# Halved, timed and held-back weight loads, fp32 edge sums for the first group and no filler products, in a graph network on one core

## The chip, the core and the metric

The kernel runs on one NeuronCore of a Trainium2 chip. The metric is the device time of one execution in microseconds (us); less is better. Before the change it is 2111.45 us, the median of three runs (2111.43 to 2111.92). Engines have short names here: PE is TensorE (PEld its loads of stationary operands), DVE is VectorE, ACT is ScalarE, POOL is GpSimd and SP is SyncE, whose queue issues all transfers.

## The reference

There are 128 graphs of 128 nodes with 256 features each, and an integer adjacency matrix per graph. Two blocks follow each other, each on normalised input and each added to its input:

```
h = relu(layernorm(x));  A = (adj != 0)
for i in 0..2:                                  # gated graph network
    aggr = A^T (h @ weight[i])
    gi = aggr @ w_ih.T + b_ih;  gh = h @ w_hh.T + b_hh
    r, z = sigmoid(...);  n = tanh(i_n + r * h_n)
    h = (1 - z) * n + z * h
x = x + h
h = relu(layernorm(x));  Wh = h @ W             # attention
e = leaky_relu(s_row + s_col),  s = Wh.sum(-1);  e = -inf where adj == 0
x = x + softmax(e) @ Wh
```

Inputs and outputs are fp32.

## The kernel before

The graphs go through in 32 groups of four. A group passes three GRU layers and then the attention block. A layer needs the edge sums of its state (A times h, `edge_sums`), and twelve gate products with weights that are composed once at the start: w_ih times each layer's message weight (L443, one compose product per 256 or 512 columns) gives `s_x0` to `s_x2`, and w_hh gives `s_hh`. The gate products use sums and differences of 128-wide blocks (`block_sums` for weights, `node_sums` for data), so seven block products stand for eight. PE's `L693` rows are the gate products of layers 0 and 1, `L700` those of layer 2.

All work is first recorded as nodes, with an engine, an estimated duration, dependences and a due time (`op`, L68). `Plan.run` then plays a schedule: each engine takes, of the nodes that can start first, the one with the smallest rank, and the order it finds is the order in which every engine's instructions are issued. Each engine works through its queue strictly in that order. So a changed estimate or due time moves instructions on all engines. Buffers come from small pools: PSUM has eight banks, of which two, called `misc`, serve short jobs such as transposes, edge sums and composes; a product into a bank waits until the bank's last content was copied out by ACT or DVE.

The start (`weights`, L378 on): SP loads w_ih (768 KB) in one transfer, the first group's rows, w_hh (768 KB), the message weights (256 KB each), adjacency blocks (256 KB) and more rows (512 KB). PE transposes the weights in blocks of 128 (`turned`, L348, three transposes into one bank; L430 for message weights), DVE or ACT copy them out (L355), composes follow. Two products of the identity (L313) fill two banks before that and are used for nothing else; they are called dummy products below. DVE takes the statistics of the rows (L512, L519), POOL the inverse root (L525, L526), DVE the shift `nm` (L528), ACT applies them (L534). DVE turns adjacency into bf16 zeros and ones (L905); the integer block has a single buffer, so the next adjacency transfer waits for that step.

The edge sums multiply by A, which is exact in bf16. The fp32 state is split into three bf16 parts whose sum is exact: for row-form states `parts_of` (POOL, L595 and L598) makes the second and third part, and each sum is three bf16 products (L635).

The end: the last two groups' attention has short steps on all engines. In group 30 ACT takes exponentials (L1010), PE transposes them (L1028), ACT copies (L1030), PE sums weighted rows (L649), ACT copies (L654), PE multiplies by W (L1041) and DVE scales and adds (L1046). The last group is handled in two halves of two graphs: PE transposes h (L1069), ACT copies (L1072), PE multiplies by W (L1078), ACT copies (L1081), and in `by_graph` follow exponentials (L1010), transposes (L1094), DVE copies (L1096), products (L1098) and the final sums (L1101), each graph written out on its own (L1104).

Between these stand filler products. `warm` (L487 to L503) records, for steps of the last two groups, a product with the step's result and then products of the identity with itself, all into bank `x_n` after the last gates; nothing reads them. They are recorded with `late=True`, which is a due time after all others, so that PE takes them only where the planner sees it idle. In the profile they are the rows of L499.

Of the kernel before, what the change touches and what calls it, by code (L numbers as in the profile page):

```python
# [16 lines left out]
P = 128  # L17
G = 4
EPS = 1e-5
ALPHA = 0.2  # L20
SETS = 4
EARLY = 3
ENDING = 2
EARLY_Z = 2
SLOT = 18150
MARGIN = 7000
GATES = 18150
BIG = 3.0e38
# [10 lines left out]
class Plan:  # L39
# [27 lines left out]

    def op(self, eng, ns, fn, reads=(), writes=(), room=(), due=None, mark=None, late=False,  # L68
           turn=None, two=False, lag=None):

        i, deps = len(self.nodes), set()
        for b in room:
            if b.prev is not None:
                deps.update(a[0] for a in b.prev.accesses)
        for is_write, group in ((False, reads), (True, writes)):
            for item in group:  # L80
                b, lo, hi = item if isinstance(item, tuple) else (item, 0, 1 << 30)
                for j, w, l, h in b.accesses:
                    if (w or is_write) and l < hi and lo < h:
                        deps.add(j)
                if is_write and b.prev is not None:
# [12 lines left out]
        self.nodes.append([eng, ns, fn, deps, free, 10 ** 9 if late else self.due if due is None else due,  # L98
                           two or eng == "POOL", self.LAG[eng] if lag is None else lag])
# [114 lines left out]
def kernel(  # L214
# [80 lines left out]
    def ap(b):  # L295
        return phys[(b.tag,) + b.slot]
# [32 lines left out]

    def load(dst, get, src, ns=100):  # L330
        op("SP", ns, lambda: nc.sync.dma_start(get(dst), src), [], [dst])

# [7 lines left out]
    def turned(src, dst, evict):  # L340

        for k in range(KD):
            for a in range(2):
                ps = bank()

                def turn(k=k, a=a, ps=ps):
                    for c in range(3):
                        nc.tensor.transpose(flat(ps)[:, c * P:(c + 1) * P],  # L348
                                            nat(src)[:, 3 * a + c, k * P:(k + 1) * P], ident)
                op("PE", 330, turn, [src], [ps])  # L350
                to_sbuf(evict[(2 * k + a) % len(evict)], 3 * P, ps, dst[k], 3 * P * a)

# [24 lines left out]
    def weights():  # L377
# [4 lines left out]
        def square(b):  # L382
            return plain(b).rearrange("p (k e) -> p k e", k=KD)

        def load_msg(layer):
            op("SP", 1300, lambda: nc.sync.dma_start(
                square(w_msg[layer]), weight[layer].rearrange("(k p) e -> p k e", p=P)),
               [], [w_msg[layer]])


        plan.due = -10 ** 6
        load(w_ih_nat, nat, w_ih.rearrange("(c p) e -> p c e", p=P), 4000)
        load_msg(0)
        plan.due = 10 ** 9
        load(w_hh_nat, nat, w_hh.rearrange("(c p) e -> p c e", p=P), 4000)
        load_msg(1)
        for t, src in (("bias_i", b_ih), ("bias_h", b_hh)):
            load(W[t], ap, src.rearrange("(c p) -> p c", p=P), 500)

# [20 lines left out]
        for layer in range(L):  # L420
# [4 lines left out]
            for e in range(KD):  # L425
# [7 lines left out]
                to_sbuf("ACT", D, ps, wT, half * GN + e * D)  # L433
            if layer == 0:
                load_msg(2)
            w_x = homes[layer]
            for k in range(KD):
                for g0, gn in ((0, 512), (512, 3 * D - 512)):
# [10 lines left out]
                    to_sbuf("DVE", gn, ps, w_x[k], g0)  # L449
            block_sums(w_x, W[f"s_x{layer}"], *(("POOL", 1000) if layer else ("DVE", 560)))  # L450

        tmp = [buf("e"), buf("e"), buf("eT")]
        for t, i, b in ((tmp[0], 0, b_ih), (tmp[1], 0, b_hh), (tmp[2], 0, b_hh), (tmp[2], 1, b_ih)):
            n = t is tmp[2]
            op("SP", 500, lambda t=t, i=i, b=b, n=n: nc.sync.dma_start(
                plain(t)[:, i * D:(i + (1 if n else 2)) * D],
                (b[2 * D:] if n else b[:2 * D]).rearrange("(o c) -> o c", o=1)
                .to_broadcast([P, D if n else 2 * D])), [], [(t, i, i + 1)])  # L460

# [24 lines left out]

    def warm(t, ns, get=None):  # L487


        if plan.group < NG - 2:  # L490
            return
        if not after_gates:
            phase_now, plan.phase = plan.phase, len(turns)
            after_gates.append(buf("x_n"))
            plan.phase = phase_now
        b = after_gates[0]

        def product(what):
            nc.tensor.matmul(flat(b)[:, :what.shape[1]], ident, what, start=False, stop=False,  # L499
                             skip_group_check=True)  # L500
        op("PE", 60, lambda: product(get() if get else plain(t)[:, :P]), [t, b], [], late=True)
        for _ in range(ns // 224):
            op("PE", 224, lambda: product(ident), [t, b], [], late=True)  # L503

    after_gates = []

    def normed(src, dst, lo=0, hi=G):
# [3 lines left out]
        for b in range(lo, hi):  # L511
            op("DVE", 415, lambda b=b: nc.vector.bn_stats(ap(st)[:, b, :], ap(src)[:, b, :]),  # L512
               [(src, b, b + 1)], [(st, b, b + 1)])
            if dst is not src and plan.group == NG - 1:
                warm((st, b, b + 1), 330, lambda b=b: ap(st)[:, b, :])

# [3 lines left out]
        op("DVE", 160 * (hi - lo), aggr, [st], [mv])  # L520
        if dst is not src and plan.group == NG - 1:
            warm(mv, 1100, lambda: ap(mv)[:, lo, :])

        def rstd():
# [5 lines left out]
           [mv, rs], [nm])  # L530
        if dst is not src and plan.group == NG - 1:
            warm(nm, 440, lambda: ap(nm)[:, part])
        for b in range(lo, hi):
# [4 lines left out]
    def flat(b):  # L538
        return ap(b).rearrange("p q n -> p (q n)")
# [86 lines left out]
    def edge_sums(parts, a, dst):  # L626

        part, reads = parts
# [267 lines left out]
    def group(g):  # L896
# [3 lines left out]
        rows0, at, a, hT = buf("rows"), buf("at"), buf("a"), buf("hT")  # L900
        op("SP", 100, lambda: nc.sync.dma_start(ap(rows0), x[graphs].rearrange("b n d -> n b d")),
           [], [rows0])
        op("SP", 100, lambda: nc.sync.dma_start(ap(at), adj[graphs].rearrange("b n m -> n b m")),
           [], [at])
        op("DVE", 420, lambda: nc.vector.tensor_scalar(ap(a), ap(at), 0.0, None,  # L905
# [31 lines left out]
    def attention(g, a, x1, h1, lo, hi):  # L937
# [8 lines left out]
        for b in range(lo, hi):  # L946
            warm((h1, b, b + 1), 440, lambda b=b: ap(h1)[:, b, :8])
            hw = buf("hw")
# [47 lines left out]
        else:  # L996
# [5 lines left out]
           [e], [top])  # L1002
        warm(top, 110, lambda: small(top))
        op("DVE", 150, lambda: nc.vector.tensor_scalar(
            small(low), small(top), -BIG / 1e3, -1.0, op0=OP.max, op1=OP.mult), [top], [low])
        warm(low, 330 * n, lambda: small(low))

# [145 lines left out]
```

## Time and profile before

| | us |
|---|---|
| median of the runs | 2111.45 |
| profiled execution | 2111.13 |
| its span, first to last instruction | 2109.1 |
| PE busy | 2098.9 |
| DVE busy | 1670.6 |
| ACT busy | 1592.1 |
| POOL busy | 940.9 |

The profile's page gives busy times, a chain of work that ended last (followed back from the last instruction), and the costliest groups of instructions. Its trace can be asked for the chain in order of time (start, length, what), for a timeline (start, length, engine, line, operation, output and input, and in brackets the idle time before it and what ended that), and for busy times by stretch. The granted PE clock is 1.000 in the whole span, and the 16 transfer engines moved 137.22 MB at a mean of 65 GB/s, but 145 GB/s in the first fortieth.

| stretch, us | PE busy | DVE busy | ACT busy | GB/s |
|---|---|---|---|---|
| 0 to 5 | 3.64 | 0.09 | 1.28 | 157 |
| 5 to 10 | 3.37 | 2.59 | 0.96 | 348 |
| 10 to 15 | 5.00 | 3.90 | 4.44 | 279 |
| 15 to 20 | 4.27 | 4.99 | 1.03 | 244 |
| 20 to 25 | 4.95 | 2.78 | 2.15 | 95 |
| 25 to 30 | 3.60 | 4.86 | 4.35 | 195 |

### The profile page before, as it was taken

Reading aid. Unit: us, or ns where it says so; the run is one execution under the profiler, and the core shown is the slowest. Engines: PE = TensorE matmul, PEld = TensorE weight load, DVE = VectorE, ACT = ScalarE, POOL = GpSimd, SP = SyncE. Lnnn points to the kernel's source line nnn. Section 1 sums busy time; section 2 is a strip of 40 time slices with the busy share of each in tenths; the row PEclk is TensorE's granted clock in tenths of the full one; section 3 lists DMA queues with packets and bytes.
Section 4 is the critical chain, followed back from the end, with each engine's and each line's share of the span. In section 5 each row is a group of like instructions: output and inputs, shape, how many; then the busy total and the mean of one; then the engine's idle time right before and its main releaser. Section 6 shows DMA issues by size and latency. Waiting matters only on the chain.

```text
span 2109.1 us, 34171 instructions
## 1 busy us (share of the span) xinstructions
PE 2098.9 (100%) x12536; PEld 1877.7 (89%) x12536; DVE 1670.6 (79%) x3365; ACT 1592.1 (75%) x2849; POOL 940.9 (45%) x885
## 2 busy tenths in 40 slices
PE   9999999999999999999999999999999999999999
PEld 7888888898888998898988889988889988988889
DVE  7777888887877888877888778878777887878777
ACT  5567878777877777777778787777777777776775
POOL 5544544445443445544354434454444444335330
PEclk9999999999999999999999999999999999999999
DMA  4222223323333222333222332223332223312321
GB/s 145 46 51 46 55 57 75 61 58 68 68 73 76 51 64 65 68 81 66 58 58 68 73 77 59 56 70 69 73 73 53 59 60 78 68 48 47 79 66 36
DMA packets 365143, 137.22 MB, mean 65 GB/s; under 512 B 296368, under 2 KB 364720, under 8 KB 364976
## 3 DMA queue, kind: packets, MB, share of 16 engines
q1 hardware_dynamic: 364976, 135.05, 29.0%
q8 instruction: 98, 1.61, 0.3%
q14 instruction: 69, 0.57, 0.1%
HBM read 45.36 MB, written 16.78 MB: 29 GB/s over the span
## 4 chain that ended last, share of the span: by engine, by line
PE 97%; DVE 1%; DMA 1%; ACT 0%; issue 0%; SPq 0%; DVEq 0%
PE y_rz L693 16%; PE q_rz L693 10%; PE x_rz L693 10%; PE y_n L693 8%; PE y_rz L700 8%; PE misc L635 6%; PE x_n L693 5%; PE q_rz L700 5%; PE q_n L693 5%; PE x_rz L700 5%; PE misc L1041 5%; PE y_n L700 4%; PE x_n L700 3%; PE q_n L700 3%; PE misc L649 2%; PE x_n L499 1%
## 5 line engine op out<-in xcount | busy, mean ns | idle before, releaser
L595 POOL TENSOR_TENSOR r<-rows 128x512 f32<-128x512 f32 x128 | 139.1, 1107 | 270.8 <-ACT rows L578 183.3
L732 ACT COPY t_rz<-y_rz 128x512 f32<-128x512 f32 x192 | 112.5, 586 | 178.1 <-PE y_rz L693 89.9
L620 POOL TENSOR_TENSOR pl<-d,pl 128x512 bf16<-128x512 f32 x64 | 74.9, 1173 | 296.5 <-ACT pl L618 296.2
L742 DVE TENSOR_TENSOR t_rz<-t_rz,q_rz 128x512 f32<-128x512 f32 x192 | 131.3, 684 | 92.9 <-ACT t_rz L732 53.7
L693 PE MATMUL y_rz<-hs,s_hh 128*128 128x256 f32 x768 | 197.6, 380 | 0.3 <-ACT t_rz L732 0.3
L693 PE MATMUL y_rz<-gs,s_x 128*128 128x256 f32 x768 | 197.1, 379 | 0.0
L667 POOL TENSOR_TENSOR hs<-hT,hs 128x256 f32<-128x256 f32 x96 | 81.7, 851 | 240.8 <-PE q_n L700 172.5
L663 POOL TENSOR_TENSOR hs<-hT 128x512 f32<-128x512 f32 x96 | 130.2, 1356 | 96.6 <-ACT hT L578 32.1
L693 PEld LDWEIGHTS y_rz<-gs,s_x 128*128 128x128 f32 x768 | 145.9, 190 | 19.8
L693 PEld LDWEIGHTS y_rz<-hs,s_hh 128*128 128x128 f32 x768 | 143.1, 190 | 19.7 <-issue 1.0
L598 POOL TENSOR_TENSOR p<-r 128x512 bf16<-128x512 f32 x128 | 154.9, 1230 | 0.0
L742 DVE TENSOR_TENSOR t_n<-t_n,q_n 128x512 f32<-128x512 f32 x192 | 131.3, 684 | 21.4 <-ACT t_n L732 8.7
L693 PE MATMUL x_rz<-hT,s_hh 128*128 128x256 f32 x512 | 131.5, 379 | 0.0
L693 PE MATMUL x_rz<-aT,s_x 128*128 128x256 f32 x512 | 131.4, 379 | 0.0
L512 DVE BATCH_NORM_STATS2 st<-rows 128x6 f32<-128x256 f32 x128 | 45.2, 414 | 101.3 <-DMA rows<-in_x_dram 101.2
L638 ACT COPY aT<-misc 128x512 f32<-128x512 f32 x192 | 111.8, 584 | 15.2 <-PE misc L635 11.3
L815 DVE TENSOR_TENSOR d<-hT,u 128x512 f32<-128x512 f32 x128 | 110.7, 865 | 10.9 <-ACT u L812 10.8
L693 PE MATMUL y_n<-hs,s_hh 128*128 128x256 f32 x384 | 114.4, 379 | 0.0
L693 PE MATMUL y_n<-gs,s_x 128*128 128x256 f32 x384 | 114.2, 379 | 0.0
L1041 PE MATMUL misc<-w,uT 128*128 128x256 f32 x480 | 113.1, 380 | 0.3 <-ACT uT L654 0.3
L615 POOL TENSOR_TENSOR d<-hT,pl 128x512 f32<-128x512 f32 x64 | 91.3, 1428 | 45.4 <-ACT pl L613 39.6
L693 PEld LDWEIGHTS x_rz<-aT,s_x 128*128 128x128 f32 x512 | 97.2, 190 | 13.2
(279 smaller groups left out, 6540.2 us busy)
## 6 DMA issues: line engine op xcount, KB each, us to landing
rows<-in_x_dram SPq DMA_DIRECT2D x32, 512.0 KB, 4.1
x<-in_x_dram SPq DMA_DIRECT2D x32, 512.0 KB, 3.9
out_dram<-x SPq DMA_DIRECT2D x31, 512.0 KB, 2.9
at<-in_adj_dram SPq DMA_DIRECT2D x32, 256.0 KB, 2.8
plT<-pl SPq DMA_TRANSPOSE x186, 3.5
peT<-pe SPq DMA_TRANSPOSE x60, 3.1
rz<-in_L_gnn_w_ih_dram SPq DMA_DIRECT2D x1, 768.0 KB, 5.0
rz<-in_L_gnn_w_hh_dram SPq DMA_DIRECT2D x1, 768.0 KB, 7.6
```

The lines of the kernel that those rows point to most:

```text
L595: op("POOL", 1106, lambda part=part: nc.gpsimd.tensor_tensor(ap(r1)[:, part], ap(rows)[:, part], top(rows)[:, part], OP.subtract), [(rows, ...
L598: op("POOL", 1050, lambda part=part: nc.gpsimd.tensor_tensor(ap(p3)[:, part], ap(r1)[:, part], top(r1)[:, part], OP.subtract), [(r1, n, n ...
L615: op("POOL", 1150, lambda k=k, r=r: nc.gpsimd.tensor_tensor(ap(r), ap(hT)[:, k], part(pl, k, 0), OP.subtract), [(hT, 2 * k, 2 * k + 2), (p ...
L635: nc.tensor.matmul(flat(ps)[:, b * N:(b + 1) * N], part(i, b, k), ap(a)[:, b, :], start=(i == 0), stop=(i == 2))
L638: op("ACT", 590, lambda k=k, ps=ps: nc.scalar.copy(ap(dst)[:, k, :], flat(ps)), [ps], [(dst, 2 * k, 2 * k + 2)])
L663: op(eng, cost, lambda: sub(ap(w)[:, 0:2, :], blocks()[:, 1::2, :], blocks()[:, 0:2, :], OP.subtract), [t], [(w, 0, 2)], two=True)
L693: nc.tensor.matmul(ap(bank)[:, half, :], ap(w)[:, i - 1, q, :], source(t, sums), start=(first and c == 0 and m == 0), stop=False, skip_gro ...
L700: nc.tensor.matmul(ap(bank)[:, m, half * P:(half + len(chunk)) * P], source(t, sums)[:, m * N:(m + 1) * N], ap(w)[:, i - 1, q:q + len(chun ...
L732: op("ACT", 590, lambda: nc.scalar.copy(ap(t), ap(y)), [y], [t], mark=mark)
L742: op("DVE", 690, lambda: nc.vector.tensor_tensor(ap(t), ap(t), ap(q), OP.add), [q], [t])
L815: op("DVE", 690, lambda j=j, d=d, cols=cols: nc.vector.tensor_tensor(ap(d), ap(hT)[:, j, :], ap(u)[:, cols], OP.subtract), [(hT, lo, hi), ...
L1041: nc.tensor.matmul(ap(ps)[:, b, :], ap(uT)[:, k, (m + b) * N:(m + b + 1) * N], ap(w1)[:, k, :], start=(k == 0), stop=(k == KD - 1))
```

## The change

Four things are changed. (1) w_ih is loaded in two transfers of 384 KB, and each transpose group needs only its half; `turned` takes the halves as the outer loop. (2) Loads are recorded with an estimate by size (`KB` = 3 ns per KB, and 3300 ns until they land) instead of a fixed one, for weights and for the first four groups' rows and adjacency. The second message weight gets an early due time; the third, the bias rows and the attention weight are recorded as depending on composed weights (`behind`), which holds back their place in SP's queue. (3) The first group's layer-0 edge sums are fp32 products of the rows with an fp32 copy of A, made by DVE (`whole_sums`), without the split into three parts. (4) `warm` and all its calls are gone.

```diff
-    def load(dst, get, src, ns=100):
-        op("SP", ns, lambda: nc.sync.dma_start(get(dst), src), [], [dst])
+    def load(dst, get, src, kb, behind=()):
+        op("SP", kb * KB, lambda: nc.sync.dma_start(get(dst), src), behind, [dst], lag=3300)
...
-        for k in range(KD):
-            for a in range(2):
+        for a in range(2):
+            for k in range(KD):
...
-                op("PE", 330, turn, [src], [ps])
-                to_sbuf(evict[(2 * k + a) % len(evict)], 3 * P, ps, dst[k], 3 * P * a)
+                op("PE", 330, turn, [(src, a, a + 1)], [ps])
+                to_sbuf(evict[k % len(evict)], 3 * P, ps, dst[k], 3 * P * a)
...
-        plan.due = -10 ** 6
-        load(w_ih_nat, nat, w_ih.rearrange("(c p) e -> p c e", p=P), 4000)
+        plan.due = -10 ** 9
+        for a in range(2):
+            part = slice(3 * a, 3 * a + 3)
+            op("SP", 384 * KB, lambda part=part: nc.sync.dma_start(
+                nat(w_ih_nat)[:, part], w_ih.rearrange("(c p) e -> p c e", p=P)[:, part]),
+               [], [(w_ih_nat, a, a + 1)], lag=3300)
         load_msg(0)
         plan.due = 10 ** 9
-        load(w_hh_nat, nat, w_hh.rearrange("(c p) e -> p c e", p=P), 4000)
+        load(w_hh_nat, nat, w_hh.rearrange("(c p) e -> p c e", p=P), 768)
+        plan.due = -10 ** 8
         load_msg(1)
+        plan.due = 10 ** 9
...
-            if layer == 0:
-                load_msg(2)
...
+            if layer == 0:
+                load_msg(2, [W["s_x0"]])
...
-                .to_broadcast([P, D if n else 2 * D])), [], [(t, i, i + 1)])
+                .to_broadcast([P, D if n else 2 * D])), [W["s_x1"]], [(t, i, i + 1)])
...
-        load(W["w1"], ap, w_att.rearrange("(k p) e -> p k e", p=P), 1300)
+        load(W["w1"], ap, w_att.rearrange("(k p) e -> p k e", p=P), 256, [W["s_x1"]])
...
-    def warm(t, ns, get=None):
...
-            warm((h1, b, b + 1), 440, lambda b=b: ap(h1)[:, b, :8])
...
+    def whole_sums(rows, a32, a, dst):
+        op("DVE", 420, lambda: nc.vector.tensor_copy(ap(a32)[:, :, :N], ap(a)), [a], [a32])
+        for k in range(KD):
+            ps = buf("misc")
+            def edges(k=k, ps=ps):
+                for b in range(G):
+                    nc.tensor.matmul(flat(ps)[:, b * N:(b + 1) * N], ap(rows)[:, b, k * P:(k + 1) * P],
+                                     ap(a32)[:, b, :N], start=True, stop=True)
+            op("PE", 880, edges, [rows, a32], [ps], [dst])
+            op("ACT", 590, lambda k=k, ps=ps: nc.scalar.copy(ap(dst)[:, k, :], flat(ps)),
+               [ps], [(dst, 2 * k, 2 * k + 2)])
...
-                parts = parts_of(rows0)
+                parts = parts_of(rows0) if g >= WHOLE else (rows0, buf("r1"))
```

More of the change, by code (lines that the diff above doesn't have):

```diff
@@ L21 @@
 SETS = 4
+WHOLE = 1
 EARLY = 3
@@ L26 @@
 MARGIN = 7000
+TIMED = 4
+KB = 3
 GATES = 18150
@@ L66, in buf, with op @@
         return b
-    def op(self, eng, ns, fn, reads=(), writes=(), room=(), due=None, mark=None, late=False,
+    def op(self, eng, ns, fn, reads=(), writes=(), room=(), due=None, mark=None,
            turn=None, two=False, lag=None):
@@ L97, in op @@
             b.left += 1
-        self.nodes.append([eng, ns, fn, deps, free, 10 ** 9 if late else self.due if due is None else due,
+        self.nodes.append([eng, ns, fn, deps, free, self.due if due is None else due,
                            two or eng == "POOL", self.LAG[eng] if lag is None else lag])
@@ L383, in square, with load_msg @@
             return plain(b).rearrange("p (k e) -> p k e", k=KD)
[L385 to L388, printed above, removed]
-        plan.due = -10 ** 6
-        load(w_ih_nat, nat, w_ih.rearrange("(c p) e -> p c e", p=P), 4000)
+        def load_msg(layer, behind=()):
+            load(w_msg[layer], square, weight[layer].rearrange("(k p) e -> p k e", p=P), 256,
+                 behind)
+        plan.due = -10 ** 9
[4 more added lines that the diff above has]
+               [], [(w_ih_nat, a, a + 1)], lag=3300)
         load_msg(0)
         plan.due = 10 ** 9
-        load(w_hh_nat, nat, w_hh.rearrange("(c p) e -> p c e", p=P), 4000)
+        load(w_hh_nat, nat, w_hh.rearrange("(c p) e -> p c e", p=P), 768)
+        plan.due = -10 ** 8
         load_msg(1)
+        plan.due = 10 ** 9
         for t, src in (("bias_i", b_ih), ("bias_h", b_hh)):
-            load(W[t], ap, src.rearrange("(c p) -> p c", p=P), 500)
+            load(W[t], ap, src.rearrange("(c p) -> p c", p=P), 100)
         def half_bias():
@@ L456, in weights @@
             n = t is tmp[2]
-            op("SP", 500, lambda t=t, i=i, b=b, n=n: nc.sync.dma_start(
+            op("SP", 150 * KB * (1 if n else 2), lambda t=t, i=i, b=b, n=n: nc.sync.dma_start(
                 plain(t)[:, i * D:(i + (1 if n else 2)) * D],
                 (b[2 * D:] if n else b[:2 * D]).rearrange("(o c) -> o c", o=1)
-                .to_broadcast([P, D if n else 2 * D])), [], [(t, i, i + 1)])
+                .to_broadcast([P, D if n else 2 * D])), [W["s_x1"]], [(t, i, i + 1)])
         def halves(t, j):
@@ L484, in weights @@
         to_sbuf("ACT", D, ps, W["w1_sum"], 0)
-    def warm(t, ns, get=None):
[L490 to L505, printed above, removed]
     def normed(src, dst, lo=0, hi=G):
@@ L513, in normed @@
                [(src, b, b + 1)], [(st, b, b + 1)])
-            if dst is not src and plan.group == NG - 1:
-                warm((st, b, b + 1), 330, lambda b=b: ap(st)[:, b, :])
         def aggr():
@@ L520, in normed @@
         op("DVE", 160 * (hi - lo), aggr, [st], [mv])
-        if dst is not src and plan.group == NG - 1:
-            warm(mv, 1100, lambda: ap(mv)[:, lo, :])
         def rstd():
@@ L530, in normed @@
            [mv, rs], [nm])
-        if dst is not src and plan.group == NG - 1:
-            warm(nm, 440, lambda: ap(nm)[:, part])
         for b in range(lo, hi):
@@ L626, in edge_sums @@
     def edge_sums(parts, a, dst):
+        if isinstance(parts[0], Buf):
+            whole_sums(*parts, a, dst)
+            return
         part, reads = parts
@@ L900, in group @@
         rows0, at, a, hT = buf("rows"), buf("at"), buf("a"), buf("hT")
[L901 to L904, printed above, removed]
+        for t, src, kb in ((rows0, x[graphs].rearrange("b n d -> n b d"), 512),
+                           (at, adj[graphs].rearrange("b n m -> n b m"), 256)):
+            if g < TIMED:
+                load(t, ap, src, kb)
+            else:
+                op("SP", 100, lambda t=t, src=src: nc.sync.dma_start(ap(t), src), [], [t])
         op("DVE", 420, lambda: nc.vector.tensor_scalar(ap(a), ap(at), 0.0, None,
@@ L1002, in attention @@
            [e], [top])
-        warm(top, 110, lambda: small(top))
         op("DVE", 150, lambda: nc.vector.tensor_scalar(
             small(low), small(top), -BIG / 1e3, -1.0, op0=OP.max, op1=OP.mult), [top], [low])
-        warm(low, 330 * n, lambda: small(low))
         def exps(lo=lo, hi=hi):
```

## The prediction

> **What bounds the kernel now.** I read the page's busy times, then its chain, then the two ends as chain and timeline.
>
> ```profile
> PE 2098.9 (100%) x12536; PEld 1877.7 (89%) x12536; DVE 1670.6 (79%) x3365; ACT 1592.1 (75%) x2849; POOL 940.9 (45%) x885
> ...
> PE 97%; DVE 1%; DMA 1%; ACT 0%; issue 0%; SPq 0%; DVEq 0%
> ```
>
> TensorE is the bound: 10.2 us of the 2109.1 us span are idle. Asked in stretches, it idles 2.1 us between 80 and 2040 us, so only the ends can give time. In the changed kernel's built order TensorE's queue differs from the old one in its first 290 rows and in the last 50, and nowhere between; VectorE, ScalarE and GpSimd likewise. The chain over the first 31 us:
>
> ```profile
> 1.82 7.64 DMA rz<-in_L_gnn_w_hh_dram
> ...
> 15.99 6.73 DMA at<-in_adj_dram
> ```
>
> The reader is to see two transfers of 7 us in the chain: the weights that came third, and the second adjacency block, queued behind transfers nobody needed yet. The timeline says what TensorE lost (in brackets the idle time and its releaser):
>
> ```profile
> 9.60 0.87 PE L348 MATMUL misc<-ident,rz 128*128 128x128 f32 x3 [0.99 <-DMA rz<-in_L_gnn_w_hh_dram]
> ...
> 22.74 0.75 DVE L905 TENSOR_SCALAR a<-at 128x512 bf16<-128x512 int32 x1 [2.16 <-DMA at<-in_adj_dram]
> ...
> 27.19 1.13 PE L693 MATMUL q_rz<-gs,s_x 128*128 128x256 f32 x4 [1.40 <-DVE gs L663]
> ```
>
> The end, as chain:
>
> ```profile
> 2080.50 3.46 PE misc L1041 x16
> 2083.96 1.24 PE x_n L499 x12
> 2085.20 0.49 PE y_rz L1028 x4
> 2085.69 1.79 PE x_n L499 x16
> ...
> 2089.26 1.34 PE x_n L499 x12
> 2090.60 1.73 PE q_rz L1041 x8
> ...
> 2103.67 4.58 PE x_n L499 x42
> ```
>
> From 2083.96 to 2108.25 TensorE is never idle: 24.29 us, of which the L499 fillers are 11.61 (all their rows of the chain) and real products 12.68. The last 4.58 us are fillers alone, while the last result is written at 2104.59:
>
> ```profile
> 2083.80 0.19 ACT L1010 ACTIVATION_READ_ACCUMULATOR e<-e,low 128x1 f32 x1
> ...
> 2085.72 0.59 ACT L1030 COPY eT<-y_rz 128x512 f32<-128x512 f32 x1 [1.22 <-PE y_rz L1028]
> ...
> 2103.71 0.88 DVE L1101 SCALAR_TENSOR_TENSOR x<-q_rz,rden,x 128x256 f32<-128x256 f32 x2 [0.71 <-PE q_rz L1098]
> ```
>
> The exponentials end at 2083.99, yet their transposes (L1028) run at 2085.05, behind 1.24 us of fillers.
>
> **The end without fillers.** I follow the changed order with the old durations. L1028 starts at 2084.04 and takes 0.75 from load to end; ScalarE copies to 2085.41; the L649 sums end for ScalarE at 2086.6 and 2087.5, its two copies at 2087.24 and 2088.13. The q_rz product starts on the first copy and finishes after the second at 2089.5, q_n at 2091.2, where the old chain has 2094.05: 2.85 gained. The last group's own chain is VectorE's: nm (L528) stays at 2088.97 and 2090.21, so h is complete at 2091.5 (old 2091.86) and the L949 rows end at 2092.47 as before. This covers nothing, because TensorE arrives only at 2091.2. L1069 to L1078 (0.88 + 0.44 + 3.46, with 0.1 of waits) then end at 2096.1, old 2099.27. The first exponentials move from 2098.71 to 2095.8, the second from 2100.00 to 2096.6. The L1094, L1096, L1098 and L1101 steps keep their lengths, 3.8 to 4.1 us from the last exponential on, so the last write ends at about 2100.7, 3.9 earlier than 2104.59. The output transfer takes 1.7 us from issue to landing: 2102.4. The old span ends 0.85 after its last instruction; I add the same: 2103.25 against 2109.1, a gain of 5.8. If nothing follows the landing it is 6.6; if VectorE and ScalarE keep half of the 3.9, it is 3.9.
>
> Does TensorE stay at full pace without fillers? The granted clock is 1.00 in all rows, also where three 128x128 fp32 transposes take 0.64 (at 9.6 to 11.5) instead of the 0.33 of later ones, so the half pace has to be read from the spacing. Row: the 1.40 idle before 27.19 leaves 59% of a 3.4 us stretch busy, and the next y_rz x8 still take 1.73, full pace. My longest gap is 0.95, and the last 3.5 us are 63% busy. By the row the sum loses 0. The Trainium skill, "TensorE: Matmul & The Clock Gate", section "A second HAM failure mode: psum-queue depth-cycling", speaks against the change: short idles between groups of matmuls, frequent enough, can make the clock swing between half and full. By it one 3.4 us window after 2088 loses 1.7 and the last products 1.1: 2.8 together. I take the row.
>
> **The start, part by part.** Bytes are the same. Arrivals follow from two rows: w_ih (768 KB) was there at 5.78 and w_hh at 9.46, after 1.31 MB more, 0.35 MB/us. In the new queue order (half, half, first message weight, second, rows, w_hh, adjacency, second rows) this gives 4.65, 5.78, 6.5, 7.3, 8.8, 11.0, 11.8, 13.3. Each half costs SP one more issue of 0.5, hidden by the transfer ahead of it.
>
> The dummy products end at about 4.9, so the first half's transposes follow with no gap (old: 5.78). At half pace 8 + 4 short groups reach 9.2, with full pace from 6.5 on 8.3; I take 8.8 for the first compose product (L443). Here a second rule counts: the same page's Part 4 says that transpose-mode products don't count as busy, by which the composes too would begin at half pace, 1.7 lost. But the old trace has nothing but transposes from 9.60 to 13.8, and their spacing falls from 0.21 to 0.11 there; I take no loss.
>
> Three composes (0.87 + 1.73 + 0.87) end at 12.3, w_hh's four groups of transposes (1.33, landed at 11.0) at 13.6. Now new waits. VectorE's queue holds statistics (1.41 + 0.37), two evictions (0.40, 0.65), the adjacency conversion (0.75), the new fp32 copy (no row for it: 0.42 to 0.75 by L905 and L355; 0.45 taken), then the eviction that the next compose waits for: 14.05, 0.5 idle. Behind that copy also stands nm, so the rows are normalised at 16.0 instead of 12.6; two composes to 17.6 cover it, with 1.6 to spare; later than that, each us is lost. The two 128-wide edge sums and transposes now take turns in one bank: the first sum waits for ScalarE's copy of hT, which stands behind five weight copies, until 19.1: 1.1 idle. Edge sums: 24 bf16 products (1.34) become 8 fp32 ones, priced by L649, 0.89 for four: 1.78, 0.44 more, and not less, since L649 has the same shape; all of it lies on TensorE's path. GpSimd's four split steps (2.22 + 2.04) go, which lets it build s_hh by 19 instead of 32.5; nobody waited for that. The second adjacency block is issued once the first is converted (13.0), behind third rows and x, and lands near 18; VectorE reaches it at 19.2, so the 2.16 stall is gone. Behind its issue on SP stand two adjacency blocks, the third message weight and rows, all needed after 24. The held-back loads (biases as rows, w_att) carry no wait of their own; they only stand later. GpSimd's seeds, which need them, come after its first s_x1 work in both orders.
>
> TensorE then runs to 29.3 having done 20.9 us of work at full pace: 8.4 not worked. Old: at 27.19, with 14.45 of work (8 x 0.33, 8 x 0.11, 5.20, 0.89, 1.34, 1.73, 0.87, 0.87), 12.7 not worked. Gain 4.3, less 0.44, is 3.9. VectorE's four bias steps (L401 to L407) took 2.6 in the old trace beside long GpSimd steps; I priced them at 1.0, since GpSimd then has only short ones. If they take 2.6, the next eviction is late and up to 1.6 goes. I take 3.4, ends 1.5 (that, and the compose start at 9.2) and 4.3 (full pace early, copies at their shortest). Later cover: first split sums of layer two need a transposed plT; old landing about 63, TensorE would reach it at 67.6.
>
> **Sum.** 3.4 + 5.8 = 9.2. The profiled execution took 2111.13 (2.03 outside its span): 2101.9. The median shown is 0.32 higher: 2111.45 - 9.2 = 2102.2.
>
> **Rivals.** *New waits eat the start* (evictions, bank turns and bias steps replace the DMA waits, gain 0 to 1): 2111.45 - 5.8 - 0.5 = 2105.2. For it: six of my stations wait for VectorE or ScalarE. Against: work worth 4.3 us of compose is pulled into the hole. Chance 0.17. *The fillers lay beside the real chain* (VectorE sets the end, only the drain goes: 1.9 of 5.8, from 2109.1 to 2106.35 + 0.85): 2111.45 - 3.4 - 1.9 = 2106.2. Against: L1028 stands 1.06 behind its exponentials. Chance 0.06. *Half pace in the end, brief*: +2.8, 2105.0; chance 0.10. *Slower*: the clock falls after the first gap at 2084.5 and stays at half through the last products: their 12.7 us of work double. It decides from 9.2 us of half-paced work; in full 2102.2 + 12.7 = 2114.9. Against: dense products between 2088 and 2096. Chance 0.02. The main case has 0.65.
>
> **How the numbers follow.** The main case's ends: start 1.5 to 4.3, end 3.9 to 6.6, both rarely together: 2100.2 to 2105.2. With the first three rivals reached in part: 2099.8 to 2106.0. The measurement can tell about 0.2%, 4.2 us, from no change: below 2107.2 lie all cases but the slow one and a little of the second and third: faster 0.94, same 0.05, slower 0.01.
>
> **What would show it.** First transposes near 4.9; no VectorE wait on the adjacency; L693's q_rz with gs finished near 29 with composes of two layers behind it; no L499 rows; q_n's L1041 product ending about 2.9 earlier relative to the misc L1041 products; the span ending about 2.5 after the last VectorE step. Wrong: transposes or products of the end at doubled spacing, TensorE idle above 3 us between 13 and 30, or new idle time between 30 and 80.

## The result, and the profile after

The changed kernel takes 2104.68 us, the median of eight runs (2104.07 to 2105.61), against 2111.43 for the kernel before in the same session (eight runs, 2110.60 to 2113.46): a ratio of 0.9967, with a 95% interval of 0.9958 to 0.9976. The gain is 6.75 us where 9.2 was forecast. The time lies inside the range, but nearer to the rival in which new waits eat the start (2105.2) than to the main case (2102.2). The profiled execution took 2104.6, its span is 2102.6.

The two traces can be cut at one place: the misc products with W that follow the last gates (L1041 before, L1040 after, x16). Whatever is gained ahead of them is the start's, since TensorE idles 2.1 us between 80 and 2040 in both. Before, in TensorE's timeline:

```profile
2080.34 3.62 PE L1041 MATMUL misc<-w,uT 128*128 128x256 f32 x16
```

The span ends 28.76 after that start. After:

```profile
2078.39 3.62 PE L1040 MATMUL misc<-w,uT 128*128 128x256 f32 x16
2081.85 0.60 PE L1027 MATMUL y_rz<-ident,e 128*128 128x128 f32 x4
...
2097.80 1.13 PE L1097 MATMUL q_rz<-d,eT 128*128 128x256 f32 x4 [0.67 <-DVE eT L1095]
```

They start at 2078.39, so **the start gained 1.95** (forecast 3.4), and the span ends 24.2 later, so **the end gained 4.5** (forecast 5.8). The transposes L1027 now follow the products at once, where fillers stood between, and the last sums (L1097) have kept their pace (1.13 with an idle time ahead of them, 1.03 before without one). The last result, in VectorE's timeline, is written 21.46 after the cut; before it was 24.25:

```profile
2098.97 0.88 DVE L1100 SCALAR_TENSOR_TENSOR x<-q_rz,rden,x 128x256 f32<-128x256 f32 x2 [0.64 <-PE q_rz L1097]
```

The start, in TensorE's timeline (start, length, what, and in brackets the idle time and what ended it):

```profile
4.86 0.49 PE L351 MATMUL misc<-ident,rz 128*128 128x128 f32 x3
...
7.57 0.41 PE L438 MATMUL misc<-ident,e 128*128 128x128 f32 x2 [1.24 <-DMA e<-in_L_gnn_weight_dram]
...
12.64 0.52 PE L351 MATMUL misc<-ident,rz 128*128 128x128 f32 x3 [0.24 <-DMA rz<-in_L_gnn_w_hh_dram]
...
25.64 1.13 PE L449 MATMUL misc<-x,uT 128*128 128x256 f32 x4 [0.93 <-DVE h L358]
...
30.18 0.66 PE L530 MATMUL misc<-ident,rows 128*128 128x128 f32 x4 [0.83 <-DVE h L358]
30.68 1.03 PE L693 MATMUL q_rz<-gs,s_x 128*128 128x256 f32 x4
```

The first transposes follow the dummy products without a gap, and TensorE is at full pace: 0.33 from one group to the next, where the old trace had 0.64 (half pace). But then it waits 1.24 for the first message weight, due at 6.5 by the forecast and there at 7.57, and later twice for VectorE, 0.93 and 0.83, waits that the forecast did not have: both are for copies of h (L358) out of a bank. In VectorE's timeline:

```profile
10.25 1.41 DVE L500 BATCH_NORM_STATS2 st<-rows 128x6 f32<-128x256 f32 x4 [3.65 <-DMA rows<-in_x_dram]
...
13.30 0.43 DVE L907 TENSOR_SCALAR a<-at 128x512 bf16<-128x512 int32 x1 [0.46 <-DMA at<-in_adj_dram]
...
26.22 1.22 DVE L663 TENSOR_TENSOR gs<-aT 128x512 f32<-128x512 f32 x1 [0.23 <-ACT aT L638]
27.47 1.15 DVE L665 TENSOR_TENSOR gs<-gs,aT 128x256 f32<-128x256 f32 x1
28.65 1.15 DVE L667 TENSOR_TENSOR gs<-aT,gs 128x256 f32<-128x256 f32 x1
```

The first rows are there at 10.25 (forecast 8.8), the first adjacency block at 13.3 (forecast 11.8), and the three gs steps (`node_sums` of the edge sums, L663 to L667) take 3.52 together. The forecast's sum has no term for them; in the old trace they took 2.98 (0.68, 1.15 and 1.15), but no copy that TensorE waited for stood behind them. From 13.30 to 30.14 VectorE has next to no idle time, and the copies of h stand in its queue: in this stretch TensorE waits for VectorE, as the forecast did not foresee. The product with gs starts at 30.68.

My first theory after the result: the start's gain is the half pace that is avoided (groups of three transposes at 0.64 instead of 0.33, and what follows them, about 3) plus the adjacency stall, less late arrivals and slow VectorE steps; the end's gain is 2.8 of path and the rest fillers that ran on after the last result. The rivals: the fp32 sums make the start's gain; the load order makes it; the fillers held up nothing, and only their run after the last result goes.

### The profile page after: what moved, and what is told of

Its sections match the earlier page's. It is cut to its first block, busy times and chain, and to the rows that moved or that the text cites. A ratio compares the mean times of both kernels' runs of the same rounds, so it can differ in the third digit from the quotient of the medians.

```text
span 2102.6 us, 33942 instructions
## 1 busy us (share of the span) xinstructions
PE 2086.2 (99%) x12422; PEld 1865.9 (89%) x12422; DVE 1668.9 (79%) x3366; ACT 1590.5 (76%) x2849; POOL 938.0 (45%) x881
## 4 chain that ended last, share of the span: by engine, by line
PE 97%; DVE 2%; ACT 1%; DMA 0%; issue 0%; SPq 0%; DVEq 0%; ACTq 0%
PE y_rz L693 16%; PE q_rz L693 11%; PE x_rz L693 10%; PE y_n L693 8%; PE y_rz L700 8%; PE misc L620 6%; PE x_n L693 5%; PE q_n L693 5%; PE q_rz L700 5%; PE x_rz L700 5%; PE misc L1040 5%; PE y_n L700 4%; PE x_n L700 3%; PE q_n L700 3%; PE misc L649 2%; DMA at<-in_adj_dram 0%
## 5 line engine op out<-in xcount | busy, mean ns | idle before, releaser
L667 POOL TENSOR_TENSOR hs<-hT,hs 128x256 f32<-128x256 f32 x96 | 82.1, 856 | 237.9 <-PE q_n L700 171.8
L663 POOL TENSOR_TENSOR hs<-hT 128x512 f32<-128x512 f32 x96 | 130.4, 1358 | 98.3 <-ACT hT L560 32.1
L1040 PE MATMUL misc<-w,uT 128*128 128x256 f32 x480 | 113.2, 380 | 0.3 <-ACT uT L654 0.3
```

The costliest lines, as they stand in the source:

```text
L663: op(eng, cost, lambda: sub(ap(w)[:, 0:2, :], blocks()[:, 1::2, :], blocks()[:, 0:2, :], OP.subtract), [t], [(w, 0, 2)], two=True)
L1040: nc.tensor.matmul(ap(ps)[:, b, :], ap(uT)[:, k, (m + b) * N:(m + b + 1) * N], ap(w1)[:, k, :], start=(k == 0), stop=(k == KD - 1))
```

## The experiments

All were timed in three sessions, each against the kernel before on the chip of that session. Its medians there are 2111.03, 2111.39 and 2111.24. "Cut" is the start of the misc products with W, "write" is the end of the last VectorE step counted from there.

**The start alone, and the fillers alone.** One kernel is the changed one with `warm` and its calls put back as they were. The other is the kernel before with one edit:

```diff
-        if plan.group < NG - 2:
-            return
+        return
```

> The changed kernel with all filler products of the last two groups put back, so only the start is changed. The change's two profiles part at the end of group 30's misc products with W: the start came 1.9 earlier there, the rest 4.6. Theory: the two parts are independent, so this kernel is 1.9 us faster than before (2109.5), its first weight transposes stand 0.33 apart and its end shows the fillers as before. Rival (the start gains nothing by itself, the offset comes from a different execution): 2111.4.

Measured 2109.17 (2107.83 to 2110.27), ratio 0.9990 (0.9982 to 0.9999): 1.86 gained. Cut 2078.32, write 24.24, as before.

> The kernel before with nothing changed but the fillers, which are left out. Theory: 4.6 us faster than before (2106.9); from the end of group 30's misc products with W to the span's end 24.0 instead of 28.6, no product at doubled spacing. Rival (the fillers kept the clock up or lay beside the path): only the drain of 1.9 to 2.3 goes, 2109.3.

Measured 2106.70 (2106.42 to 2106.99), ratio 0.9979 (0.9970 to 0.9988): 4.33 gained. Cut 2080.32, write 21.44. The two gains add up to 6.2, which is the whole change (6.75) within the scatter: the parts are independent. The fillers of the old chain last 11.6 in sum, so the larger part of them filled time in which TensorE would have waited or had nothing left to do. No product of the end has doubled spacing without them. That the write comes 2.81 earlier accounts for the larger part; the other 1.5 is what ran after the last result.

**Only the last half group's fillers left out**, in the kernel before:

```diff
-        if plan.group < NG - 2:
+        if plan.group < NG - 2 or second_half:
...
+            if (lo, hi) == (0, G // 2):
+                second_half.append(g)
             attention(g, a, x1, h1, lo, hi)
```

> The kernel before with the fillers of the very last half group left out, and all others kept. TensorE's queue then is the old one up to the last exponentials and ends with the last sums. Theory: the gain of leaving out all fillers, 4.3, is 2.8 of shorter path (last VectorE step, seen from the misc products with W: 24.25 before, 21.44 without) and 1.5 of fillers that run on after the last result. So this one gains 1.5 (2109.6) and its last VectorE step stays at 24.2. Rival (the path isn't held up by fillers, all is drain): 4.3, 2106.8.

Measured 2110.83 (2110.27 to 2112.75), ratio 0.9997 (0.9988 to 1.0006): 0.4 gained, neither theory's number. TensorE's timeline shows why:

```profile
2102.20 0.51 PE L499 MATMUL x_n<-st,ident 128*128 128x6 f32 x4
...
2103.68 1.11 PE L1100 MATMUL q_n<-d,eT 128*128 128x256 f32 x4
```

The planner moved the remaining late fillers (from L499 with `st` on, 1.5 us) ahead of the last sums, so the write comes 25.36 after the cut, 1.1 later than before; the span then ends 2.82 after the write instead of 4.51. The run after the last result is thus worth 1.7, as the theory had it, but this edit paid 1.1 of it back. So a filler in the queue ahead of the sums does cost time: here 1.5 of fillers cost 1.1. (This execution's own start ended 2.0 later than that of before, so only times from the cut on are read here.)

**fp32 edge sums: none, two groups, three groups.** One number is changed:

```diff
-WHOLE = 1
+WHOLE = 0
```

> The changed kernel with the first group's layer-0 edge sums again as three bf16 products and GpSimd's split. Theory: the start gain comes mainly from the weights' transposes at full pace (0.33 apart, about 3.2) and from the adjacency block that is no longer waited for; the split costs GpSimd 4.3, which puts s_hh later and slows VectorE's s_x0 steps beside it, against 0.4 less on TensorE: 0 to 1 us slower than the changed kernel (2104.7 to 2105.7). Rival (the fp32 sums are the start's gain): 1.9 slower or more, 2106.6.

Measured 2104.24 (2102.65 to 2105.03), 6.8 less than before. The fp32 sums are not the start's gain; with bf16 sums the kernel is as fast. In its profile the first rows are there at 8.48, not at 10.25, with the same queue order; what that means is taken up below.

> The changed kernel with fp32 edge sums for the first two groups. GpSimd then no longer splits rows (4.6 us from 25.8 to 30.7) while VectorE makes the first gs. Theory: VectorE's steps take twice as long beside GpSimd's, so the three gs steps shrink from 3.52 to about 2, TensorE's waits of 0.93 and 0.83 for VectorE before the third compose go or shrink, and 0.44 of fp32 products and 0.43 of VectorE's copy come on top: 0.3 to 1.0 us faster than the changed kernel (2104.0). Rival (VectorE's steps are slow by themselves): gs stays at 3.5 and the time rises by 0.4 to 0.9 (2105.3).

Measured 2103.80 (2102.61 to 2104.37), with WHOLE = 2. VectorE's timeline:

```profile
26.50 0.69 DVE L663 TENSOR_TENSOR gs<-aT 128x512 f32<-128x512 f32 x1
27.23 0.42 DVE L665 TENSOR_TENSOR gs<-gs,aT 128x256 f32<-128x256 f32 x1
27.69 0.42 DVE L667 TENSOR_TENSOR gs<-aT,gs 128x256 f32<-128x256 f32 x1
```

Without GpSimd's split of the second group's rows (4.6 us, from 25.8 to 30.7 after the change) the same three steps take 1.53 instead of 3.52. TensorE's wait before the second group's transposes is gone (that of 0.94 before the compose product is still there, as the split began only after it), and its product with gs starts at 29.91, though the transfers came 0.3 later in this execution. So the disputed cost is contention with GpSimd. (The trace shows it, not the median: 2103.80 and 2104.68 lie within the scatter of the two kernels.) The Trainium skill, "SBUF — State Buffer", section "Who interferes with whom", states it as a rule: a VectorE instruction with two operands in SBUF contends with a GpSimd instruction that reads SBUF. The runs agree for these steps.

> The changed kernel with fp32 edge sums for the first three groups. With two groups the first gs took 1.53 instead of 3.52, and the second gs (3.9) stood beside the third group's split on GpSimd. Theory: that goes too (second gs near 1.6), but TensorE had no wait for the second gs, and 0.44 of products comes on top: the time of two groups plus 0 to 0.5 (2104.0). Rival (each split taken from GpSimd frees the path): again 0.9 faster, 2102.9.

Measured 2104.32 (2103.93 to 2104.43), with WHOLE = 3: no further gain, as expected, though the second gs steps shrank as well (to 0.68, 0.42 and 0.42). Removing a split pays only where VectorE is what TensorE waits for.

**The changed kernel once more**, with no edit.

> The changed kernel once more. With the same first twelve transfers in the same order, the first message weight had landed at 7.6 to 7.9 in three profiles (the changed kernel, the one with fillers, the one with two groups of fp32 sums) and by 6.4 in a fourth (bf16 sums); TensorE reached its full pace at 4.9, 5.5, 5.9 and 5.9. Theory: both are drawn anew in every execution and not set by the kernel, so a new profile shows other values for both, and the times scatter by 2 us where those of before scatter by 1. Rival (the program fixes them): 7.57 and 4.86 again, to 0.1. Time by both: 2104.7.

Measured 2104.68 (2103.15 to 2104.92). TensorE's timeline:

```profile
4.93 0.85 PE L351 MATMUL misc<-ident,rz 128*128 128x128 f32 x3
...
7.96 0.41 PE L438 MATMUL misc<-ident,e 128*128 128x128 f32 x2 [0.49 <-DMA e<-in_L_gnn_weight_dram]
...
12.63 0.52 PE L351 MATMUL misc<-ident,rz 128*128 128x128 f32 x3
```

The transposes now run at half pace until about 6.9 (they start at 4.93, 5.57, 6.21 and 6.85), and yet everything from 12.63 on stands as in the first profile, and the span is 2102.8 instead of 2102.6. So the pace is indeed not fixed by the program, but the first message weight and then w_hh are later than the transposes at either pace: the half pace is hidden. My first theory fell here: in this load order it explains none of the gain. Of the arrivals, the rows (10.22) were those of the first profile, as the rival had it, and the message weight (7.96) came 0.4 later.

**w_ih in one transfer, without and with a bridge of dummy products.**

```diff
-        for a in range(2):
-            part = slice(3 * a, 3 * a + 3)
-            op("SP", 384 * KB, lambda part=part: nc.sync.dma_start(
...
+        load(w_ih_nat, nat, w_ih.rearrange("(c p) e -> p c e", p=P), 768)
```

> The changed kernel with w_ih in one transfer again, all else kept. Theory (the start's gain is that the dummy products run on into the first transposes without a gap): w_ih lands at 5.8, TensorE has a gap of 0.6 to 0.9 again, the transposes and what follows run at half pace to 9 or later, first compose product at about 10 instead of 8.8, and 1 to 2 us of the start's gain is lost: 2106. Rival (the halves matter only by the earlier landing of the first): 0 to 0.5 lost, since the first compose product waits for the first message weight at 7.6 anyhow: 2104.9.

Measured 2103.01 (2102.78 to 2106.01): faster than with halves, against both expectations. The rows are there at 8.98. The profiled execution is the slowest of its five runs (span 2104.2, the others 2100.8 to 2101.1) and the only one that went as the theory had it. TensorE's timeline there shows what half pace costs when the transfers are early enough not to hide it:

```profile
5.99 0.90 PE L351 MATMUL misc<-ident,rz 128*128 128x128 f32 x3 [0.85 <-DMA rz<-in_L_gnn_w_ih_dram]
...
10.58 1.03 PE L445 MATMUL x_rz<-x,uT 128*128 128x256 f32 x4
```

The gap of 0.85 is back, the transposes stand 0.64 to 0.70 apart, and the first compose product starts at 10.58. The second kernel adds to this:

```diff
+MORE = 3
...
+    for c in range(MORE):
+        nc.tensor.matmul(y[:, :P], ident, ident, start=False, stop=True, skip_group_check=True)
```

> The kernel with w_ih in one transfer and three more dummy products of the identity behind the others, 0.23 each at full pace and 0.47 at half, so that TensorE is busy until the transfer lands. Theory: with no gap the pace becomes full by 6.0 though the transfer comes as late as before, and the transposes stand 0.33 apart: within 0.5 of the changed kernel (2104.9), better than without these products by 1 or more. Rival (the gap doesn't set the pace): as without them, or 0.3 to 0.5 slower for the added work.

Measured 2103.35 (2103.15 to 2103.66), not below the 2103.01 without these products, but with all four spans between 2100.9 and 2101.2:

```profile
4.93 1.25 PE L319 MATMUL y_n<-ident 128*128 128x128 f32 x6
6.02 0.49 PE L354 MATMUL misc<-ident,rz 128*128 128x128 f32 x3
...
8.66 1.03 PE L448 MATMUL x_rz<-x,uT 128*128 128x256 f32 x4
```

No gap, full pace from the first transpose, first compose product at 8.66, and cut at 2076.09: 4.25 gained in the start. Against the one-transfer kernel's profiled execution that is 1.9 at the compose product and 3.1 at the cut. The 1.2 between the two is VectorE's: in the late execution all three gs steps stand beside GpSimd's split (3.78 instead of 2.98), and TensorE waits 1.34 instead of 0.20 for a copy behind them. That its other four runs were as fast as the bridged ones fits a pace that happens to rise in time in most executions; those runs have no trace, so this stays an inference.

**The bridge alone**, added to the kernel before.

> The kernel before with three more dummy products only, so that TensorE has no gap before w_ih's transposes. Theory: the pace becomes full by 6.0 and the first compose product starts at 11.5 to 12 instead of 13.79, but the second adjacency block still lands at 22.7, VectorE's queue waits for it and the gs after it still frees TensorE at 27.2: 0 to 0.7 gained (2111.0). Rival (the pace alone is worth what it costs): 2 or more, 2109.

Measured 2111.75 (2111.14 to 2112.36), ratio 1.0001 (0.9992 to 1.0009): nothing gained, though full pace was reached by the second group of transposes:

```profile
9.54 0.52 PE L351 MATMUL misc<-ident,rz 128*128 128x128 f32 x3 [2.32 <-DMA rz<-in_L_gnn_w_hh_dram]
...
27.45 1.13 PE L696 MATMUL q_rz<-gs,s_x 128*128 128x256 f32 x4 [1.44 <-DVE gs L666]
```

TensorE waits 2.32 for w_hh, and VectorE then waits 2.97 for the second adjacency block (to 23.32). The first compose product starts at 13.37 and not at 11.5 to 12, since normalised rows come first in TensorE's queue and are not ready. In the old load order, too, the half pace cost nothing.

**The old loads in the changed kernel**: `load` without size, lag and `behind`, the old estimates and due times, the halves kept.

```diff
-        op("SP", kb * KB, lambda: nc.sync.dma_start(get(dst), src), behind, [dst], lag=3300)
+        op("SP", ns, lambda: nc.sync.dma_start(get(dst), src), [], [dst])
...
-                load_msg(2, [W["s_x0"]])
```

> The changed kernel with the loads again untimed, in nearly the old order and not held back (first half, second half, w_hh, rows, first message weight, adjacency, rows), the halves, the fp32 sums and the missing fillers kept. Theory: most of the start's gain is in the order: the second adjacency block lands after 20 again, VectorE's queue waits for it by 1 to 2, and gs comes near 27 with one compose layer fewer done: 1.5 to 2 of the start's gain lost, 2106.4. Rival (the halves and the fp32 sums carry the start): the changed kernel's 2104.7 or less.

Measured 2113.68 (2112.94 to 2114.77), ratio 1.0011 (1.0004 to 1.0018): 9 us slower than the changed kernel and 2.4 slower than before. With halves the planner puts w_hh ahead of the first rows, so this order is not quite the old one. VectorE's timeline:

```profile
10.66 1.41 DVE L498 BATCH_NORM_STATS2 st<-rows 128x6 f32<-128x256 f32 x4 [3.77 <-DMA rows<-in_x_dram]
...
24.38 0.43 DVE L902 TENSOR_SCALAR a<-at 128x512 bf16<-128x512 int32 x1 [6.89 <-DMA at<-in_adj_dram]
```

The second adjacency block holds VectorE for 6.89, not for the 1 to 2 of the theory, with the compose copies queued behind it; TensorE waits 2.64 for w_hh and 2.49 for the second message weight. The 9 us are not what the old order costs: the kernel before without its fillers, in the true old order and with neither halves nor fp32 sums, took 2106.70, only 2.0 more than the changed kernel. The other 7 come with the queue that the old estimates make of the halves, above all the later second adjacency block (24.38; 22.84 there); the shares were not separated. What the run does show is that halves and fp32 sums gain nothing without the new loads. As bf16 sums and a single w_ih transfer cost nothing either (2104.24 and 2103.01), the new loads, timed and held back, are left as the start's gain. The kernel before with these alone was not run.

**The second message weight at its old place**, the changed kernel otherwise.

```diff
-        plan.due = -10 ** 8
         load_msg(1)
-        plan.due = 10 ** 9
```

> The changed kernel, halves kept, with the second message weight back at its old place in SP's queue, so that six transfers stand ahead of the second rows instead of seven. With one w_ih transfer (six ahead) the first rows had landed by 8.6 to 9.0 and the time was 2103.0 to 2103.4; with halves (seven ahead) they landed at 10.2 to 10.6 in five of six profiles and the issue of the second rows took 2.7 to 3.2 instead of 1.3 to 1.5. Theory: the number of transfers ahead sets this, not the halves; first rows by 9.0, second rows' issue at most 1.8, w_hh by 11.2, no wait of TensorE for a transfer after 7; time 2103.4 if the later composes cost nothing. Rival (a half, with rows of three pieces, is itself the slow form): first rows at 10 again, 2104.7.

Measured 2102.56 (2101.78 to 2103.03), ratio 0.9956 (0.9941 to 0.9971): the fastest of all, 8.7 ahead of the kernel before and 2.1 ahead of the changed one. The issue of the second rows on SP's queue, after the change and in this kernel:

```profile
4.61 2.93 SPq L334 DMA_DIRECT2D rows<-in_x_dram  x1
```

```profile
4.22 1.65 SPq L334 DMA_DIRECT2D rows<-in_x_dram  x1
```

The first rows and adjacency in its VectorE timeline:

```profile
8.20 1.41 DVE L498 BATCH_NORM_STATS2 st<-rows 128x6 f32<-128x256 f32 x4 [1.77 <-DMA rows<-in_x_dram]
...
11.36 0.43 DVE L905 TENSOR_SCALAR a<-at 128x512 bf16<-128x512 int32 x1 [0.90 <-DMA at<-in_adj_dram]
```

The rows come 2.05 earlier than after the change and the adjacency 1.94 earlier. Of this, 0.7 is the 256 KB that no longer stand ahead of them (by 0.35 MB/us); the other 1.2 to 1.3 is not a matter of bytes. The cut is at 2075.60: 4.74 gained in the start. GpSimd's split now falls elsewhere, and the three gs steps take 1.52.

What sets the late arrivals, then? It is not the bytes ahead of the second rows: 2816 KB with halves and with one transfer, late in the one, early in the other. It is not the halves alone: this kernel has them. The number of transfers ahead of the second rows goes with it in part. With seven ahead the first rows came at 10.1 to 10.6 in five profiles of six; the exception (bf16 sums) had them at 8.48 and an issue of 1.78 instead of 2.7 to 3.2. With six ahead they came at 8.2 to 9.0 in three profiles of four. The fourth is the kernel with the old loads: its w_hh was there at 9.27 and its rows at 10.66, where the same 0.35 MB/us gives 8.0 and 9.4, and its issue of the second rows took 2.13. So the count alone does not decide it. That one transfer fewer helped this kernel is shown; what the queue or the transfer engines do there stays open.

## Why the prediction was right, and where it was not

**Which stages could gain: right.** Only the two ends changed; the middle idles 2.1 as before.

**First transposes near 4.9, no gap: right, but worth nothing by itself.** I took 8.8 for the first compose, between 8.3 at full pace and 9.2 at half. That it came at 8.79 is luck: the pace was full, and 1.24 of waiting for the message weight made up the difference. At half pace it started at 9.18, with the same span. In the old order the bridge gained nothing either. The pace showed a price, 1.9 at the first compose and 3.1 at the cut, only in one profiled execution of the one-transfer kernel, where the arrivals were early.

**Arrivals at 0.35 MB/us, one after the other: this step failed.** The bytes moved at nearly that rate (329 GB/s between 5 and 10 us, 348 before), but message weight, rows, w_hh and adjacency came 1.1, 1.4, 1.6 and 1.5 later than the sum. I took the arrivals from the old queue and did not ask whether its rate holds for each transfer of another one. With one w_ih transfer and the bridge the sum holds: rows at 8.65 (8.8), w_hh by 11.25 (11.0). It holds as well with the second message weight late, which takes 256 KB out of it: rows at 8.2 (8.1), adjacency at 11.4 (11.1). In the other late case, the old loads in the changed kernel, it fails by 1.2 to 1.3.

**Stall on the second adjacency gone: right.** VectorE does not wait for it, where it waited 2.16 before. What such a stall can grow to shows in the kernel with the old loads: 6.89, as the late block holds all compose copies behind it in VectorE's queue.

**VectorE's gs steps: a term that was left at nothing.** My sum does not name them; they took 3.52 beside the second group's split, and 1.53 without it. I had priced the bias steps for just this effect, and they took 0.6 (no GpSimd step on a large block stood beside them), below my 1.0. The effect was right and its place wrong: it must be asked of every VectorE step once the order is known. The small waits were close: eviction 0.5 forecast and 0.64 measured, hT copy 1.1 and 0.68. So were the fp32 edge sums: 1.78 and 1.88.

**Start, 3.4 forecast, 1.95 measured.** With arrivals on time (second message weight late, or one transfer with the bridge) it is 4.7 and 4.3, at or above my upper end of 4.3. Of the two terms the arrivals are the larger: without the contention but with late arrivals (two groups of fp32 sums) the start gained 2.3, and with early arrivals and gs steps still at 2.98 (the bridge) 4.3.

**The end, 5.8 forecast, 4.5 measured, 4.3 with the fillers alone.** The mechanism held. The middle of the path is as forecast: seen from the cut, q_n's product ends 2.96 earlier (2.9). But the last write came 2.8 earlier and not 3.9. Of the 1.1, 0.5 is my own sum: I took 3.8 to 4.1 as the time from the last exponential on and added it to 2096.6, which is the start of the second pair of exponentials; from there to the last write the old trace has 4.59 (2100.00 to 2104.59). The second pair starts at 2095.07, 0.4 later than forecast (2096.6 less 1.95): a copy ahead of the exponentials in ScalarE's queue waits 0.50 for TensorE's y_rz products. The last 0.2 is a transpose whose bank waits for a VectorE copy. After the write I put 2.55 to the span's end; it was 2.75 here and 2.75 to 3.58 in the eleven profiles without any fillers or without the last half group's.

**Half pace in the end: right that it doesn't come.** All gaps there are at most 0.85, and products keep their lengths in every kernel without fillers. Its price of 2.8 was an estimate, with the 3.4 us window that the Trainium skill states in "TensorE: Matmul & The Clock Gate", Part 1. The rule that I weighed, from the same page's section "A second HAM failure mode: psum-queue depth-cycling", did not show here.

**Rivals.** "The fillers lay beside the chain" fell (4.3 gained by their removal, not 1.9). "New waits eat the start" was half right: waits did eat 1.5 of 3.4. Of the causes that it named, the evictions took part (the 0.93 and 0.83 are waits for copies of h), the bank turns and bias steps did not; late transfers and GpSimd's contention it did not name.

## What to carry to other kernels

Order the first loads by when their data is used, and look at what stands behind each wait on the waiting engine: one late block at the head of VectorE's queue held it for 6.89 us, more than the whole gain of the start. Bytes alone do not give the arrival of an urgent transfer: here one transfer fewer ahead of it was worth 2 us, though the cause is open, so try it. Fillers that keep an engine busy cost time wherever the real chain has caught up with it; take them out and look whether the pace falls. Ask of every VectorE step in a tight stretch which GpSimd step will stand beside it.

## What was not expected of the hardware

- With the same kernel, TensorE's half pace ended by 4.9 in one execution and near 6.9 in another. The Trainium skill, "TensorE: Matmul & The Clock Gate", Part 1, says that the window over which activity is watched runs free of the kernel's start, which fits. The granted clock of the profile shows 1.00 there in both; for this first stretch only the spacing of equal products tells. Later changes of pace it does show, as the next two points have it.
- A gap of 2.32 (bridge on the kernel before) left TensorE at full pace; after a gap of 2.64 (old loads in the changed kernel) the transposes stood 0.22 apart instead of 0.11 and products stayed at half pace until about 22. The granted clock is 1.00 through the first gap; around the second it goes from 1.00 (7 to 8.5) to 0.50 (9 to 22).
- In the profile with only the start changed, the last fillers themselves ran at half pace from 2105 on (128x2 products 0.57 instead of 0.36, granted clock 0.50), though TensorE had no idle time before them. The kernel before with the bridge has the same from about 2107.6 on; in the kernel before, the same fillers end at full pace.
